# A graph-attention and expert layer: edge blocks read at fixed places, more source rows gathered early

## Chip, cores and metric

The kernel runs on one core of a Trainium2 chip. The metric is the device time of one execution in microseconds (us), as the median of several runs. PE is TensorE (PEld its weight loads), DVE is VectorE, ACT ScalarE, POOL GpSimd, SP SyncE; SP and ACT issue plain DMAs, POOL the indirect ones (gathers).

## The reference, cut to what matters

30000 nodes with 256 features, 510000 edges sorted by destination, each with a source and one of 8 types. The layer norm, one graph attention over the edges, and then a feed-forward part with a shared network and four gated experts:

```python
feat_all = einsum('ni,rhid->rnhd', layernorm(x), conv_weights)   # 8 types, 4 heads of 64
feat_src_e = feat_all[edge_type, edge_src]
feat_dst_e = feat_all[edge_type, edge_dst]
e = leaky_relu(sum(feat_src_e * attn_l[edge_type]) + sum(feat_dst_e * attn_r[edge_type]))
alpha = softmax of e over the edges of each destination
x = x + segment_sum(alpha[..., None] * feat_src_e, edge_dst) + h_bias
x = x + shared(layernorm(x)) + the two best of 4 experts, weighted
```

## The kernel before, in words

**Stage A** (lines 248 to 850) makes the features of all nodes. The nodes are 235 row tiles of 128. For each tile m, `norm` makes the layer norm (DVE statistics L164 and L165, a square root on ACT L167, reciprocal L168 and scaling L171 on DVE), `turn` transposes it on PE (L322, copied out at L324), and `group` multiplies it with the weights in five column groups (L335), whose results ACT or DVE copies out of PSUM into `fo` (L337); six PSUM banks stand between PE and these copies. `store` sends 1040 KB per tile to `feat` in DRAM, on SP (L351). `fo` has six buffers. Each feature row has 4 heads of 65 numbers, the last one being the source's part of the score. The parts for the destinations go to `er_d`.

The order of the work is written out by hand: the loop at L826 goes over the tiles and groups, and each engine runs its instructions in the order in which they are issued there. Between the groups, `aside` (L811) makes one step of a list of generators, `side` (L808): six steps per tile while it is busy with the edges. These generators are:

- `edge_records` (L369): reads src, type and dst in 10 chunks of 120 x 425 edges, writes one record of 4 numbers per edge (row, destination, type, "starts a node") to `rec` in DRAM, and then finds, for each of 252 blocks, the first edge at or after 2016 t that starts a new node (`lo_sb`) and that node's number.
- `places` (L613): for 21 batches of 12 blocks it loads the 2048 edges from each block's first edge on, with the position in a register (L629, L632; every third load is issued by ACT, the others by SP), sorts the 16 edges of each partition by source with MAX8 (L561), and makes `rko`: indices, masks, penalties and bits, written to `rk_d` (`records`, L541).
- `ranks` (L674): the three lowest sources of each partition make three lists of 128 rows per block, 756 lists in all. They are ranked by their highest row, in comparisons and in matmuls with 0/1 matrices (L724, L730).
- `expert_weights`: loads for stage B.

From tile 68 on, `early_rows` (L753) gathers these lists in the order of their ranks while the later features are still being made: one indirect DMA of 128 rows each (`fr`, L765, twelve buffers), and eight lists later a plain DMA to the list's own place in `stage` (L762, by turns from SP and ACT). `PACE` spreads them over tiles 68 to 231: 4.638 lists per tile. `early(i)` (L537) says how many tiles must be stored before list i may be gathered; a list above its bound raises a flag.

**Stage B** (L1020 to L1340) goes over the 252 blocks and one last block. `load` (L1055) fetches a block's records, `gather` (L1087) fills a ring of four blocks with 16 feature rows per partition: three come from `stage` in one DMA on SP, 13 in indirect DMAs on POOL (L1095). DVE and ACT make scores, the softmax and one-hot matrices; PE sums the weighted rows per destination (L1213). Beside it, step by step, the feed-forward part runs for groups of 512 finished nodes (class `Experts`, L852).

At the end stand loops that repeat the attention in a general way. They run only if the flag `bad` is raised: when a block's first edge, a node count, the order of dst or an early list's bound breaks what the blocks take for granted.

Of the kernel before, what the change touches and what calls it, by code (L numbers as in the profile page):

```python
# [65 lines left out]
EARLY = 3  # L66
# [7 lines left out]
def kernel(  # L74
# [41 lines left out]
    assert EP * EG * GPP == E and 512 <= N < 32768 and NBLK * S + 64 <= E  # L116
# [5 lines left out]
    rec = dram.tile([E + PAD, 4], I32, name="rec")  # L122
    dst16 = dram.tile([E + PAD], I16, name="dst16")
    rk_d = dram.tile([NBLK, P, OWN.n], I32, name="rk_d")
    rl_d = dram.tile([P, LAST.n], I32, name="rl_d")
    NI = EARLY * NBLK
# [10 lines left out]
    uns_d = dram.tile([EP], F32, name="uns_d")  # L137
# [9 lines left out]
    lo_sb = const.tile([1, KT * P], I32, name="lo_sb")  # L147
# [98 lines left out]
    with ExitStack() as cx:  # L246
# [54 lines left out]
        def norm(m):  # L301
            if m >= NT:
                return
            q, j = divmod(m, T)
            t = tiles[m] = {"xn": layernorm(xp, quad[q][:, j:j + 1], 1, "a", bufs=6)}
            if j == 1:
                load_x(q + 1)

        normed = [0]

        def norms(m):
            while normed[0] <= m:
                norm(normed[0])
                normed[0] += 1
# [54 lines left out]
        def edge_records(cl):  # L369

            srcv = src.rearrange("(p c) -> p c", p=EP)
            dstv = dst.rearrange("(p c) -> p c", p=EP)
            typv = edge_type_8.rearrange("(p c) -> p c", p=EP)
            recv = rec[0:E, :].rearrange("(p c) f -> p c f", p=EP)
            d16v = dst16[0:E].rearrange("(p c) -> p c", p=EP)
            gs = max(k for k in range(1, 6) if GPP % k == 0)
            nch = GPP // gs
            n = gs * EG
            uns = gp.tile([EP, nch], F32, name="uns")
            ep = cl.enter_context(tc.tile_pool(name="edges", bufs=2))  # L380
            edges = {}

            def fetch(c):
                if c == nch:
                    return
                c0 = c * n
                s_sb = ep.tile([EP, n], I32, name="s_sb")
                nc.sync.dma_start(s_sb, srcv[:, c0:c0 + n])
                t_sb = ep.tile([EP, n], I32, name="t_sb")
                nc.sync.dma_start(t_sb, typv[:, c0:c0 + n])  # L390
                d_sb = ep.tile([EP, n + 1], I32, name="d_sb")
                if c:
                    nc.sync.dma_start(d_sb, dstv[:, c0 - 1:c0 + n])
                else:
                    nc.vector.memset(d_sb[:, 0:1], -1)
                    nc.sync.dma_start(d_sb[:, 1:], dstv[:, :n])
                    with nc.allow_non_contiguous_dma(reason="one edge of each partition, once"):
                        nc.sync.dma_start(d_sb[1:EP, 0:1], dstv[0:EP - 1, EC - 1:EC])
                edges[c] = s_sb, t_sb, d_sb

            fetch(0)
            for _ in range(3):
                yield
            for c in range(nch):
                c0 = c * n
                fetch(c + 1)
                s_sb, t_sb, d_sb = edges.pop(c)
                yield
                r_sb = ep.tile([EP, n, 4], I32, name="r_sb")
                nc.vector.scalar_tensor_tensor(r_sb[:, :, 0], s_sb, float(R), t_sb, op0=ALU.mult, op1=ALU.add)  # L410
                nc.gpsimd.tensor_copy(r_sb[:, :, 1], d_sb[:, 1:])
                nc.gpsimd.tensor_copy(r_sb[:, :, 2], t_sb)
                yield
                nc.vector.tensor_tensor(r_sb[:, :, 3], d_sb[:, 1:], d_sb[:, :n], op=ALU.not_equal)
                d16 = ep.tile([EP, n], I16, name="d16")
                nc.gpsimd.tensor_copy(d16, d_sb[:, 1:])
                yield
                dn = ep.tile([EP, n], F32, name="dn")
                nc.vector.tensor_tensor(dn, d_sb[:, 1:], d_sb[:, :n], op=ALU.is_lt)
                nc.sync.dma_start(recv[:, c0:c0 + n, :], r_sb)  # L420
                nc.sync.dma_start(d16v[:, c0:c0 + n], d16)
                yield
                nc.vector.tensor_reduce(uns[:, c:c + 1], dn, AX.X, ALU.max)
                yield
            cl.close()
            pad = gp.tile([P, PAD // P, 4], I32, name="pad")
            nc.gpsimd.memset(pad, 0)
            nc.gpsimd.memset(pad[:, :, 1], -1)
            nc.gpsimd.memset(pad[:, :, 3], 1)
            padd = gp.tile([P, PAD // P], I16, name="padd")  # L430
            nc.gpsimd.memset(padd, -1)
            zx = gp.tile([P, D], F32, name="zx")
            nc.gpsimd.memset(zx, 0.0)
            yield
            nc.sync.dma_start(rec[E:E + PAD, :].rearrange("(p u) f -> p u f", p=P), pad)
            nc.sync.dma_start(dst16[E:E + PAD].rearrange("(p u) -> p u", p=P), padd)
            for j in range(2):
                nc.sync.dma_start(er_d[N + j * P:N + j * P + P], zx[:, :R * H])
            yield


            WN = 64
            FAR = float(1 << 23)
            dw = gp.tile([P, KT, WN + 1], I32, name="dw")
            nc.gpsimd.memset(dw, -1)
# [3 lines left out]
            first = gp.tile([P, KT], F32, name="first")  # L449
# [4 lines left out]
            for k in range(KT):  # L454
                nc.vector.tensor_scalar(first[:, k:k + 1], irow, float(S), float(k * P * S), op0=ALU.mult,
                                        op1=ALU.add)
# [19 lines left out]
            nc.vector.tensor_add(lof[:, 0, :], lof[:, 0, :], first)  # L476
            nc.vector.tensor_scalar_min(lof[:, 0, :], lof[:, 0, :], float(E))
            nc.vector.tensor_scalar(lof[:, 1, :], lof[:, 1, :], 0.0, float(N), op0=ALU.max, op1=ALU.min)
            yield
            lor = gp.tile([1, KT * P], F32, name="lor")  # L480
            nr = gp.tile([1, KT * P], F32, name="nr")
# [9 lines left out]
            nc.vector.tensor_copy(lo_sb, lor)  # L491
# [5 lines left out]
            unm = gp.tile([EP, 1], F32, name="unm")  # L497
            nc.vector.tensor_reduce(unm, uns, AX.X, ALU.max)
            yield
            with nc.allow_non_contiguous_dma(reason="one number of each partition, once"):  # L500
                nc.sync.dma_start(uns_d.rearrange("(p o) -> p o", o=1), unm)
            yield
            unr = gp.tile([1, EP], F32, name="unr")
            nc.sync.dma_start(unr, uns_d.rearrange("(o p) -> o p", o=1))


            two = gp.tile([1, 6], F32, name="two")
            gap = gp.tile([1, NBLK], F32, name="gap")
            for i, (row, most) in enumerate(((lor, CAP), (nr, P))):
                nc.vector.tensor_sub(gap, row[:, 1:NBLK + 1], row[:, :NBLK])  # L510
                nc.vector.tensor_reduce(two[:, i:i + 1], gap, AX.X, ALU.max)
                nc.vector.tensor_scalar(two[:, i:i + 1], two[:, i:i + 1], float(most), None, op0=ALU.is_gt)
                yield
# [3 lines left out]
            nc.vector.tensor_reduce(two[:, 4:5], unr, AX.X, ALU.max)  # L517
# [5 lines left out]
            nc.vector.tensor_reduce(two[:, 5:6], gap, AX.X, ALU.max)  # L523
# [6 lines left out]
        far = gp.tile([P, 2], F32, name="far")  # L530
        lists = gp.tile([P, NI], I32, name="lists")
        held = gp.tile([1, NI], I32, name="held")
        AT = 68 * NT // 235 if NT >= 100 else NT
        LAG, GI = 4, 21
        PACE = NI / ((NT - 4 - AT) * NG) if AT < NT else NI
# [5 lines left out]
        def records(kp, rc, lay, o, b0, n, order):  # L541

            u, of, ob = lay.u, o.bitcast(F32), o.bitcast(BF16)
            FL = [P, n, u]
            dst0 = rc[:, :, 0:1, 1]
            kw = kp.tile([P, n, u], F32, name=f"kw{u}")
            nc.vector.tensor_tensor(kw, rc[:, :, :u, 1], dst0.to_broadcast(FL), op=ALU.subtract)
            nc.gpsimd.tensor_copy(spans[:, b0:b0 + n], kw[:, :, u - 1])
            nc.gpsimd.tensor_copy(ends[:, 2, b0:b0 + n], rc[:, :, 0, 1])
            kk = kp.tile([P, n, u], F32, name=f"kk{u}")  # L550
            nc.vector.tensor_scalar(kk, kw, 0.0, float(K - 1), op0=ALU.max, op1=ALU.min)
            vi = kp.tile([P, n, u], I32, name=f"vi{u}")
            if order:
                key = kp.tile([P, 2, n, u], F32, name=f"key{u}")
                nc.vector.scalar_tensor_tensor(key[:, 1], rc[:, :, :u, 0], float(K), kk, op0=ALU.mult, op1=ALU.add)
                nc.vector.tensor_scalar_mul(key[:, 0], key[:, 1], -1.0)
                yield
                half = kp.tile([P, 2, n, 8], F32, name=f"half{u}")
                for b in range(n):
                    for i in range(2):  # L560
# [46 lines left out]
            for i, v in enumerate((4, 2, 1)):  # L607
                nc.vector.tensor_scalar(bits[:, :, i], ty, float(v), None, op0=ALU.is_ge)
                if v > 1:
                    nc.vector.tensor_single_scalar(ty, ty, v - 1, op=ALU.bitwise_and)  # L610
# [962 lines left out]
```

## Time and profile before

| | us |
|---|---|
| median of 3 runs | 6174.72 (6170.01 to 6176.68) |
| profiled execution | 6156.64 |
| its span, first to last instruction | 6155.0 |
| PE busy | 5745.5 (93%) |
| DVE busy | 4483.9 (73%) |
| POOL busy | 3996.1 (65%) |
| ACT busy | 3448.8 (56%) |
| stage A's gathers L765 | 756, from 608.2 to 1821.9 |
| stage B's gathers L1095 | 3294, from 1857.6 to 6017.7 |
| last matmul of stage A ends | 1852.1 |

The page gives busy times over the whole span, the span in 40 slices, the DMA queues, the chain that ended last and the costliest groups of instructions. The stages have different limits, so the table of windows (busy time of each engine in a stretch) and the waits of a stretch are of more use than the whole span's shares. An engine's idle time says nothing by itself; what matters is which wait ends last in a stage.

### The profile page before, as it was taken

To read this page: it belongs to the slowest core of one execution; us is meant where nothing else is said; L and a number is where in the kernel's file an instruction comes from. 1 tells how busy PE (TensorE), PEld (TensorE's weight loads), DVE (VectorE), ACT (ScalarE), POOL (GpSimd) and SP (SyncE) were. 2 spreads that over 40 slices of the span, in tenths; PEclk is the share of its full clock that TensorE was granted. 3 is DMA by queue.
4 is the path that set the end of the run, shared out by engine and by line. 5 is a ranking of instruction groups with operands and counts; after the bars stand their busy time and mean duration, and the time that the engine had idled before them with its cause. 6 is when DMAs were issued, how large, how long until landed. Compare 5 with 4: busy or idle time off the path is not lost. (4 is left out here: it accounts for less than half of the span.)

```text
span 6155.0 us, 91629 instructions
## 1 busy us (share of the span) xinstructions
PE 5745.5 (93%) x21807; PEld 3671.0 (60%) x21808; DVE 4483.9 (73%) x12808; ACT 3448.8 (56%) x8892; POOL 3996.1 (65%) x4365
## 2 busy tenths in 40 slices
PE   8789999999995899999999999999999999999998
PEld 4445555555553566666666666666666666666665
DVE  5673333333336888888888888888888888888884
ACT  3232222222224677677776677677677776677764
POOL 2230456566657777777777777777777777777770
PEclk9999999999997899999999999999999999999999
DMA  7574899999985666666666656665666656656551
GB/s 255 178 242 163 302 334 337 336 335 336 333 310 164 172 174 174 175 172 171 176 173 176 174 171 173 174 174 170 177 172 175 175 171 176 174 170 176 174 169 38
DMA packets 750202, 1257.46 MB, mean 204 GB/s; under 512 B 160453, under 2 KB 566017, under 8 KB 719441
## 3 DMA queue, kind: packets, MB, share of 16 engines
q0 software_dynamic: 194400, 539.40, 32.0%
q1 hardware_dynamic: 487681, 658.52, 31.5%
q10 hardware_dynamic: 67568, 53.54, 2.7%
q8 instruction: 180, 2.95, 0.2%
q14 instruction: 373, 3.06, 0.1%
HBM read 806.71 MB, written 444.28 MB: 203 GB/s over the span
## 5 line engine op out<-in xcount | busy, mean ns | idle before, releaser
L1095 POOL DMA_INDIRECT ft<-feat,rk x3294 | 3157.8, 959 | 1037.9 <-issue 381.7
L1213 PE MATMUL po<-ft,oh 128*128 128x260 f32 x8100 | 2160.2, 407 | 0.0
L1213 PEld LDWEIGHTS po<-ft,oh 128*128 128x128 f32 x8100 | 1540.3, 200 | 561.4 <-issue 272.4
L335 PE MATMUL ps<-w,xT 128*128 128x448 f32 (+1 forms) x4700 | 1736.8, 524 | 69.3 <-ACT fo L337 37.0
L335 PEld LDWEIGHTS ps<-w,xT 128*128 128x128 f32 x4700 | 882.0, 192 | 778.7 <-issue 614.4
L1149 ACT ACTIVATE oh<-icol,rk 128x128 f32<-128x128 f32 x4050 | 1334.8, 390 | 0.0
L1206 DVE TENSOR_TENSOR ft<-ft,p 128x768 f32<-128x768 f32 x1518 | 1278.8, 853 | 2.7 <-ACT ft L1199 2.7
L765 POOL DMA_INDIRECT fr<-feat,lists x756 | 716.1, 947 | 644.6 <-DMA stage<-fr 305.6
L337 ACT COPY fo<-ps 128x448 f32<-128x448 f32 (+1 forms) x808 | 413.1, 528 | 1072.0 <-PE ps L335 577.5
L1150 ACT ACTIVATE oh<-oh 128x384 f32<-128x384 f32 x1518 | 740.3, 488 | 48.1
L1132 DVE COPY_PREDICATED ere<-rk,pe 128x512 f32<-128x512 int16 (+1 forms) x759 | 549.1, 723 | 187.3 <-ACT ere L1127 178.6
L1198 ACT ACTIVATE p<-e 128x64 f32<-128x64 f32 (+1 forms) x253 | 71.2, 281 | 852.0 <-DVE e L1193 851.8
L951 PE MATMUL ph<-xT,v 128*128 128x512 f32 (+1 forms) x944 | 446.7, 597 | 0.0
L324 DVE COPY xT<-ptr 128x256 f32<-128x256 f32 x181 | 76.9, 425 | 467.1 <-PE ptr L322 467.1
L337 DVE COPY fo<-ps 128x256 f32<-128x256 f32 (+1 forms) x367 | 192.3, 524 | 282.7 <-PE ps L335 262.8
L895 PE MATMUL ph<-ident,c_xn 128*128 128x128 f32 x470 | 141.4, 374 | 141.8 <-ACT c_xn L887 138.1
L1139 DVE COPY_PREDICATED ere<-rk,ere 128x256 f32<-128x256 int16 (+1 forms) x759 | 247.7, 326 | 17.4
L1102 PE MATMUL t<-ident,tops 128*8 128x128 f32 x506 | 100.6, 282 | 160.2 <-DVE tops L1163 160.1
L951 PEld LDWEIGHTS ph<-xT,v 128*128 128x128 f32 x944 | 170.5, 190 | 123.6 <-issue 113.1
L1013 PE MATMUL pf<-v,a 128*128 128x256 f32 x940 | 242.0, 380 | 0.1
L951 PE MATMUL ph<-xT,w 128*128 128x512 f32 (+1 forms) x472 | 230.0, 610 | 0.2 <-ACT xT L897 0.2
L1277 DVE SCALAR_TENSOR_TENSOR xt<-po,den,xt 128x64 f32<-128x64 f32 x1012 | 217.4, 277 | 9.0
(239 smaller groups left out, 6059.5 us busy)
## 6 DMA issues: line engine op xcount, KB each, us to landing
feat<-fo SPq DMA_DIRECT2D x234, 1040.0 KB
ft<-stage SPq DMA_DIRECT2D x252, 390.0 KB
ft<-feat,rk POOLq DMA_INDIRECT x3294
stage<-fr SPq DMA_DIRECT2D x378, 130.0 KB
stage<-fr ACTq DMA_DIRECT2D x378, 130.0 KB
xt<-in_x_dram SPq DMA_DIRECT2D x253, 128.0 KB
x_d<-xt SPq DMA_DIRECT2D x253, 128.0 KB
x<-x_d SPq DMA_DIRECT2D x58, 512.0 KB
```

The lines of the kernel that those rows point to most:

```text
L335: nc.tensor.matmul(ps, t["xT"][:, k, :], w[:, k, c0:c1], start=k == 0, stop=k == 1)
L337: eng(t["fo"][:, h0:h1, :HD], ps[:, :n].rearrange("p (a d) -> p a d", d=HD))
L765: nc.gpsimd.indirect_dma_start(out=fr, out_offset=None, in_=feat[0:min(early(i // GI * GI) * P, N) * R, :], in_offset=bass.IndirectOffsetO ...
L951: nc.tensor.matmul(ps[:, :self.w], lhs, rhs, start=i == 0, stop=i == len(pairs) - 1)
L1013: nc.tensor.matmul(pf[:M], self.a2[:, i, tok], v3[:, i, :], start=False, stop=False)
L1095: nc.gpsimd.indirect_dma_start(out=s.ft[:, u].rearrange("p h d -> p (h d)"), out_offset=None, in_=feat[:, :], in_offset=bass.IndirectOffse ...
L1132: nc.vector.copy_predicated(s.ere, s.mask[:, k - 1, :, None].to_broadcast(at), s.pe[:, k:k + 1].to_broadcast(at))
L1139: nc.vector.copy_predicated(s.ere[:, :, :n], s.bits[:, i, :, None].to_broadcast([P, s.u, n]), s.ere[:, :, n:2 * n])
L1149: nc.scalar.activation(s.oh[:, u, :], icol, AF.Abs, bias=s.nd[:, u:u + 1])
L1150: nc.scalar.activation(s.oh[:, u0:u1], s.oh[:, u0:u1], AF.Relu, bias=1.0, scale=-1.0)
L1206: nc.vector.tensor_mul(fc, fc, pc[:, :, None].to_broadcast([P, (u1 - u0) * H, HD]))
L1213: nc.tensor.matmul(s.po.rearrange("n h d -> n (h d)"), s.oh[:, u, :], s.ft[:, u].rearrange("p h d -> p (h d)"), start=u == 0, stop=u == s. ...
```

## The change

- `edge_records` and the records in DRAM go (they are made only inside the loops at the end). `ordered`, a new generator, reads src, type and dst of 12 blocks at a time directly, at fixed places: block t always reads the 2048 edges from 2016 t on, the destinations with one neighbour on either side. All these loads are issued by SP. It sorts the 16 edges of each partition and keeps the sorted values `vi` and the destinations `dk` (16 bit) in SBUF, and the lowest rows for the lists. `borders` finds the first nodes of the blocks, one step for every four of `ordered`.
- `ranks` comes next, before `places`. Its 0/1 selections are made per half of the columns (441) and used at once by two matmuls.
- `places` finishes the records afterwards, from `vi` and `dk`, in 28 turns of 9 blocks; flags that were read from the records are now compared from neighbouring destinations. `rk_d` is laid out by partition: a turn writes 4608 bytes per partition in one piece.
- Lists: four per even block and three per odd block, 882 in all, from tile 60 on and up to tile 233: 5.098 per tile. Stage B gathers 12 rows per partition of an even block and 13 of an odd one.
- The statistics of a row tile are made in three slots of the loop (sums at group 0, square root at group 1, reciprocal and scaling at group 3) instead of all at group 1. The double step of `aside` moves from group 3 to group 2.

```diff
-EARLY = 3
+EARLY = 7
+def firsts(b):
+    return b // 2 * EARLY + b % 2 * 4
...
-    rk_d = dram.tile([NBLK, P, OWN.n], I32, name="rk_d")
+    rk_d = dram.tile([P, NBLK, OWN.n], I32, name="rk_d")
-    NI = EARLY * NBLK
+    NI = firsts(NBLK)
...
         def norm(m):
+            nc.vector.bn_stats(st, xg)
+            nc.vector.bn_aggr(mv, st)
+            yield
+            nc.scalar.activation(rs, mv[:, 1:2], AF.Sqrt, bias=eps)
+            yield
+            nc.vector.reciprocal(rs, rs)
+            nc.vector.tensor_scalar(xn[:, 0], xg, mv[:, 0:1], rs, op0=ALU.subtract, op1=ALU.mult)
...
-        AT = 68 * NT // 235 if NT >= 100 else NT
+        AT = 60 * NT // 235 if NT >= 100 else NT
-        PACE = NI / ((NT - 4 - AT) * NG) if AT < NT else NI
+        PACE = NI / ((NT - 2 - AT) * NG) if AT < NT else NI
...
+        def ordered(cl):
+                s = kp.tile([P, GB, U], I32, name="s_in", bufs=3)[:, :n]
+                nc.sync.dma_start(s, window(src, b0 * S, n, U))
+                t = kp.tile([P, GB, U], I32, name="t_in", bufs=3)[:, :n]
+                nc.sync.dma_start(t, window(edge_type_8, b0 * S, n, U))
+                    nc.sync.dma_start(d, window(dst, b0 * S - 1, n, U + 2))
+                nc.vector.tensor_tensor(kw, d[:, :, 1:U + 1], d[:, :, 1:2].to_broadcast([P, n, U]), op=ALU.subtract)
+                nc.gpsimd.tensor_copy(dk[:, b0:b0 + n], d)
+                nc.vector.tensor_scalar(kk, kw, 0.0, float(K - 1), op0=ALU.max, op1=ALU.min)
+                nc.vector.scalar_tensor_tensor(row, s, float(R), t, op0=ALU.mult, op1=ALU.add)
+                nc.vector.scalar_tensor_tensor(key[:, 1], row, float(K), kk, op0=ALU.mult, op1=ALU.add)
+                        nc.vector.max(half[:, i, b], key[:, i, b])
...
+        def mixed(cl):
+            other = borders()
+            for i, _ in enumerate(ordered(cl)):
+                yield
+                if i % 4 == 3:
+                    next(other, None)
...
         def places(cl):
-                    eng, dma = (ACT, nc.scalar) if b % 3 == 2 else (SP, nc.sync)
-                    dma.dma_start(rc[:, b].rearrange("p u f -> p (u f)"),
-                                  bass.AP(tensor=r.tensor, offset=r.offset, ap=[[4 * U, P], [1, 4 * UW]]))
-            for k, (b0, n) in enumerate(batches):
+            for k, (b0, n) in enumerate(turns):
+                for i, _ in enumerate(records(kp, OWN, o, vi[:, b0:b0 + n], dk[:, b0:b0 + n], k, b0, n)):
...
         def ranks(cl):
+                for c in range(IC):
+                    place = rp.tile([P, half], F32, name="place", bufs=3)[:IS, :n]
+                    nc.vector.tensor_scalar(place, order[:IS, i:i + n], rank[:, c:c + 1], None, op0=ALU.is_equal)
+                    nc.tensor.matmul(pl, turn_r[:, c], place, start=c == 0, stop=c == IC - 1)
+                    nc.tensor.matmul(pn, number[:, c:c + 1], place, start=c == 0, stop=c == IC - 1)
...
-            side = [edge_records(cl), places(cl), ranks(cl), expert_weights()]
+            side = [mixed(cl), ranks(cl), places(cl), expert_weights()]
...
-                        norms(m + NORMED)
-                    for _ in range((2 if g == 3 else 1) if busy else g == 2):
+                    if g in (0, 1, 3):
+                        norm_part()
+                    for _ in range((2 if g == 2 else 1) if busy else g == 2):
...
         def gather(t):
-                i, n = EARLY * t, EARLY
+                i, n = firsts(t), firsts(t + 1) - firsts(t)
```

## Prediction

> **What bounds the kernel now.** I read the table of windows first, because the kernel has two stages with different limits and shares over the whole span mix them. Columns: window, its length, then busy time and count for PE, PEld, DVE, ACT, POOL, then granted PE clock, DMA share, GB/s.
>
> ```profile
> 0.00:193.00 193.00, 150.76 (x415) 78.53 (x417) 93.82 (x222) 53.55 (x160) 34.58 (x63) 0.92 0.68 222
> 193.00:453.00 260.00, 221.61 (x622) 114.76 (x620) 218.79 (x1180) 80.50 (x257) 84.41 (x211) 0.95 0.71 223
> 453.00:508.00 55.00, 51.75 (x153) 27.05 (x154) 23.67 (x53) 16.98 (x53) 2.73 (x38) 0.93 0.60 189
> 608.00:1852.00 1244.00, 1244.00 (x3744) 675.76 (x3742) 467.10 (x1510) 320.62 (x677) 716.08 (x756) 1.00 0.94 326
> 2000.00:6018.00 4018.00, 3789.42 (x15863) 2596.68 (x15862) 3502.13 (x9345) 2827.82 (x7377) 3048.93 (x3182) 0.95 0.60 173
> 6018.00:6155.00 137.00, 111.78 (x427) 68.57 (x425) 50.09 (x161) 59.72 (x130) 1.12 (x4) 0.91 0.08 28
> ```
>
> From 608 to 1852 PE is busy all the time at full clock: stage A (the feature matmuls) is PE's. From 2000 to 6018 PE has gaps and a clock of 0.95, while POOL shows 76%. Which of them leads is told by POOL's timeline (start, length, idle before) and by the groups of its gather line:
>
> ```profile
> 1949.81 0.94 POOL L1095 DMA_INDIRECT ft<-feat,rk  x1 [0.30 <-PE t L1182]
> 1951.06 0.95 POOL L1095 DMA_INDIRECT ft<-feat,rk  x1 [0.30 <-DMA ft<-feat,rk]
> 1952.31 1.12 POOL L1095 DMA_INDIRECT ft<-feat,rk  x1 [0.30 <-issue]
> ...
> L1095 POOL DMA_INDIRECT ft<-feat,rk x3294: 940/946/1262, 1857.6 to 6017.7; - x194
> ```
>
> The gap before each gather is 0.30 us whatever the view names as its releaser, so POOL waits for nobody: 3293 steps from 1857.6 to 6017.7 are 1.2633 us each, 13 of them 16.42 us per block. POOL's gathers bound stage B; PE runs dry behind them, and after a dry spell its clock drops. The kernel is stage A until 1857.6, then 3294 gathers, then a tail of 137 us.
>
> In stage A the timeline of PE shows one transposition per row tile, 7.31 us apart wherever nothing disturbs it:
>
> ```profile
> 57.88 0.38 PE L322 MATMUL ptr<-ident,a_xn 128*128 128x128 f32 x2
> ...
> 65.19 0.38 PE L322 MATMUL ptr<-ident,a_xn 128*128 128x128 f32 x2
> ```
>
> 235 tiles at 7.31 are 1718 us; PE ends at 1852, so 134 us are lost, all before 520. The starts of these transpositions place the loss: tiles 8 to 16 lose 11, tiles 17 to 19 35, tiles 20 to 47 (193 to 453, `places`) 56, tiles 48 to 53 (`ranks`) 22, of which 17 are its own matmuls; the first 47 us lose some 10. The waits say why, first 47 to 193, then 193 to 453 (total, times, longest):
>
> ```profile
> ACT a_rs L167 <- DVE a_mv L165: 97.1, 15, 16.1
> PE ps L335 <- ACT fo L337: 34.0, 8, 12.0
> ```
> ```profile
> ACT fo L337 <- DMA rcb<-rec: 107.7, 16, 9.6
> ACT a_rs L167 <- DVE a_mv L165: 40.9, 14, 5.2
> DVE a_rs L168 <- ACT a_rs L167: 34.9, 29, 7.7
> PE ps L335 <- ACT xT L324: 29.1, 12, 4.7
> ```
>
> ACT, which empties PE's banks, stands behind DVE's statistics and behind loads of `rcb` that it issues itself; in 193 to 453 DVE is busy 218.8 and waits 34.9 for ACT's square root, together 253.7 of 260. DVE sets that stretch.
>
> **The change, part by part.** Sums are against the profiled execution: 6156.64 us, span 6155.0. The median of the runs is 18 us above it; I move the sum onto the median unchanged.
>
> *Gathers of stage B.* 756 staged lists become 882, so 126 gathers leave L1095: 12.5 per block, 3168 in all. 126 x 1.2633 = 159 us off the queue that bounds. Next in line is PE. At full clock the 100 us windows of stage B hold 418 to 435 matmuls, against 397 on average (14704 in 3700 us); a block has 65.3, so PE needs 15.0 to 15.6 us where POOL will need 12.5 x 1.2633 = 15.79. DVE is busy 87%, 14.3 us of a block. POOL stays last, by a thin 0.2 to 0.8 us. Bounds of this gain: 0 (PE keeps 16.42) to 159; I take 159, as PE's dips follow its own dry spells. Stage reads grow from 390 to 455 KB per block, at a DMA share of 0.60; hidden.
>
> On the clock the trace has a row: after PE's 2.07 us wait for c_xn at 2687 its next pair takes 0.96 us instead of 0.47. The Trainium skill, "TensorE: Matmul & The Clock Gate", Part 1, lets the clock fall after an idle window of some 3.4 us. By that rule only the 4 to 6 us gaps would cost, and they go when POOL is faster; by the row the c_xn gaps cost as well and PE sits nearer to 15.8. The sum is 159 by either.
>
> *Early lists in stage A.* They run from tile 60 to 233 at 5.098 per tile, where it was 4.638. POOL then needs 5.098 x 1.25 = 6.4 of 7.31 us: room. DMA has less:
>
> ```profile
> 700.00:1800.00 1100.00, 1100.00 (x3312) 597.70 (x3311) 418.23 (x1355) 285.48 (x603) 661.00 (x698) 1.00 0.97 336
> ```
> ```profile
> GB/s 319 352 341 341 320 345 341 317 338 346 335 340 333 341 343 316 335 341 332 336 336 341 320 351 329 337 342 336 344 325 338 334 342 324 328 347 327 338 340 338
> ```
>
> A tile moves 1.212 MB (features out, x in, er out) and 0.266 MB per list: 2.447 MB in 7.31 us is 335 GB/s, the 336 shown. After: 2.570 MB, 351 GB/s. Slices of 27.5 us reach 352 and average 336. If 352 can be held, nothing is lost; if 336 is the ceiling, a tile takes 7.65 us and 173 tiles lose 58. I take the middle, 344: 7.47 us, 27 us lost; call it 30. A late list holds ACT (it issues half of the writes to `stage`, L762), ACT holds the copies L337, and PE's six banks fill.
>
> A ceiling is also on a page: the Trainium skill, "DMA: Bandwidth & Descriptors", Specifications, gives about 358 GB/s of HBM per core. By it 351 just fits and the sum would be 30 us lower; the share of 0.97 at 336 speaks for less.
>
> *Edge preparation.* Records written and read back go; src, type and dst are loaded directly as 3 x 252 x 128 = 96768 packets of 64 and 72 bytes. The trace's packet records have 38-byte packets at 10.9 ns and 128-byte ones at 12.7; at 11.5 that is 70 us of the 16 engines in some 21 tiles (154 us), beside feature stores of 43%. Bounds: 0 lost, or at 24 ns each (the 256-byte packets at the start) 145 us plus stores, 57 lost. I take 0: the near sizes lie close. The 84 loads on ACT's queue go, and with them its 107.7 us of waiting; all new ones stand on SP's queue, ahead of feature stores, which six buffers cover. `borders` now advances every fourth step, so its DMA round trips no longer stop DVE as at 140 to 190.
>
> Steps: 129 for sorting, 31 for `ranks`, 194 for `places`, six per tile: 59 tiles, where it was 48. Sorting costs DVE per tile: three tensor-tensor forms 0.50+0.45+0.43, two scalar forms 0.52, 24 MAX8 at 0.082, halves and low rows 0.53, sum 4.4, with the statistics (0.42+0.18+0.16+0.43) 5.6 of 7.31: PE leads. A turn of `places` (9 blocks, one tile), scaled from the rows of 12 blocks: 12 scalar forms at 0.23 to 0.28 (3.0), 9 small ones at 0.16 to 0.2 (1.7), four others 1.5: 6.2, with statistics 7.4. Against 7.31 that is 28 x 0.1 = 3 us, as long as the square root no longer stops DVE: sum and reciprocal now lie two slots apart, ACT's part between. If that cover fails, 1 us per tile comes back, 30 us.
>
> So: tiles 8 to 19 keep 15 of 46; `places` keeps 20 of 56 (3, the tail with `thr` 7, slip 10); `ranks` goes from 22 to 28 (28 products of 441 columns for 24 of 378, and PE now waits on DVE's selections one at a time, with the tile's own matmuls queued behind and ACT's copies behind those). Net 59 us gained; bounds 0 and 95.
>
> **Sum.** -159 + 30 - 59 = -188: 5969 against the profiled execution, 5987 on the median.
>
> **Rivals.**
> 1. *PE takes over in stage B.* For it: a margin of 0.2 to 0.8 us per block, c_xn gaps that halve the clock. Against: POOL never waits. If half is lost: -80 + 30 - 59 = -109, 6066. Chance 0.15.
> 2. *The early part gains nothing* (small packets, or DVE as slow as before): -159 + 30 = -129, 6046. Chance 0.10.
> 3. *No loss on DMA*: -218, 5957. Chance 0.12.
> 4. *Slower: DMA overload stops PE in every tile.* Lists land late, ACT blocks, PE pauses, the clock halves. To eat 218 us of gain each of 173 tiles must lose 1.26 us, 8.57 us per tile, which is 300 GB/s; from there on it is slower. At 1.5 times that loss the time is 6284. Against: 336 are held now. Chance 0.04, and 0.02 for landing within 0.2% either way.
> 5. *It doesn't do what it says*: a border over 32 edges, or a list over its bound, raises the flag, and the loops at the end repeat the attention: at least stage B's 4160 us more. From the inputs the largest border is 29 and the nearest list 9 tiles inside. Chance 0.02.
>
> **How the numbers follow.** The forecast has 0.55. Measurements of this kernel tell 0.2% (12 us) from no change. Faster: 0.55 + 0.15 + 0.10 + 0.12 = 0.92; within 0.2%: 0.02; slower: 0.06. The range runs from both good bounds (-159 - 95 + 0, 5921) to rival 1 with the DMA ceiling at 336 (-81, 6094).
>
> **What would show it.** Right: gaps before L1095's successor stay 0.30 us with 3168 of them; tiles in 193 to 450 near 7.5 us; no ACT wait for edge loads; DMA near 0.99 between tiles 60 and 233 and the last transposition some 30 us earlier than now. Wrong: POOL waiting on PE's `po` for whole microseconds; tiles above 7.6 us in the middle of stage A; PE waits on `place` beyond 10 us.

## The result, and the profile after

| | us |
|---|---|
| changed kernel, median of 4 runs | 31232.61 (31215.06 to 31247.23) |
| kernel before, same chip | 6172.36 (6168.76 to 6176.68) |
| ratio | 5.0598, 95% interval 5.051 to 5.0686 |
| forecast | 5987 (5921 to 6094) |

The change made the kernel five times slower. The table of windows of the changed kernel (columns as in the prediction) shows two parts:

```profile
1000.00:1780.00 780.00, 780.00 (x2349) 424.45 (x2348) 276.85 (x949) 190.22 (x423) 515.77 (x545) 1.00 1.01 351
...
2200.00:5800.00 3600.00, 3414.77 (x14293) 2340.21 (x14292) 3142.34 (x8391) 2544.21 (x6631) 2618.32 (x2736) 0.95 0.60 173
...
6200.00:31200.00 25000.00, 15283.82 (x76360) 13109.28 (x76360) 9776.35 (x25852) 1307.86 (x3689) 4875.17 (x4703) 0.70 0.15 39
```

Up to about 6070 us the profile is of the kind shown before; the timeline has the last store of the normal output at 6070.27. Then come 25000 us of another program: PE at 0.70 of its clock, DMA at 0.15. The costliest groups of the page name it:

```profile
L1506 POOL DMA_INDIRECT ft<-feat,rc x4700 | 4874.7, 1037 | 17661.7 <-SPq L1566 13542.8
...
L1543 PE MATMUL pb<-ident,e 128*128 128x128 f32 x37600 | 7024.1, 345 | 0.0
```

Lines 1506 and 1543 stand in the loops at the end, which run only if `bad` is raised. So it was raised. The 4700 gathers there fetch the rows of all edges a second time, one group of four after the other, with POOL idle 17662 us between them.

The normal part did not go as forecast either. Its gathers, and the waits from 2200 to 5800 us (total, times, longest):

```profile
L1119 POOL DMA_INDIRECT ft<-feat,rk x3168: 940/946/1266, 1796.1 to 5943.4; - x198
```
```profile
POOL ft L1119 <- PE po L1237: 277.2, 726, 3.4
...
PE ph L919 <- ACT c_xn L911: 116.1, 122, 2.1
```

There are 126 gathers fewer, as said, but they take 4147 us where 3294 took 4160. And POOL now waits for PE by up to 3.4 us, where no such wait exceeded 0.3 before. The prediction had listed this as a sign that it is wrong.

### The profile page after: what moved, and what is told of

Its sections match the earlier page's. It is cut to its first block, busy times and chain, and to the rows that moved or that the text cites. A ratio compares the mean times of both kernels' runs of the same rounds, so it can differ in the third digit from the quotient of the medians.

```text
span 31232.9 us, 358971 instructions
## 1 busy us (share of the span) xinstructions
PE 21050.5 (67%) x98275; PEld 16796.5 (54%) x98276; DVE 14295.1 (46%) x38991; ACT 4774.5 (15%) x12655; POOL 8885.5 (28%) x9179
## 3 DMA queue, kind: packets, MB, share of 16 engines
q0 software_dynamic: 420000, 1165.36, 13.7%
## 5 line engine op out<-in xcount | busy, mean ns | idle before, releaser
L1506 POOL DMA_INDIRECT ft<-feat,rc x4700 | 4874.7, 1037 | 17661.7 <-SPq L1566 13542.8
L1543 PEld LDWEIGHTS pb<-ident,e 128*128 128x128 f32 x37600 | 6832.9, 257 | 1222.1 <-issue 886.7
L1543 PE MATMUL pb<-ident,e 128*128 128x128 f32 x37600 | 7024.1, 345 | 0.0
L1540 PE MATMUL pb<-msk,identb 128*128 128x512 bf16 x4700 | 2294.1, 488 | 4810.2 <-DVE mc L1546 1927.0
L1522 PE MATMUL pe<-er,ohT 128*128 128x33 f32 x9400 | 1753.4, 333 | 3277.5 <-DVE ohT L1511 3127.3
L1522 PEld LDWEIGHTS pe<-er,ohT 128*128 128x128 f32 x9400 | 1662.1, 259 | 3547.4 <-DVE ohT L1511 3370.0
L1546 DVE TENSOR_REDUCE mc<-pb 128x4 f32<-128x2048 f32 x1175 | 2692.4, 2291 | 1476.9 <-PE pb L1543 1476.9
L1561 PE MATMUL po<-ft,oh 128*128 128x260 f32 x9400 | 3007.5, 476 | 430.4 <-issue 430.4
L1561 PEld LDWEIGHTS po<-ft,oh 128*128 128x128 f32 x9400 | 2318.8, 252 | 909.6 <-issue 444.1
L1237 PE MATMUL po<-ft,oh 128*128 128x260 f32 x8100 | 2163.8, 407 | 0.0
L1554 PE MATMUL pq<-mc,ohT 128*128 128x4 f32 x9400 | 1569.8, 290 | 627.8 <-DVE mc L1547 627.8
L1237 PEld LDWEIGHTS po<-ft,oh 128*128 128x128 f32 x8100 | 1544.6, 200 | 558.1 <-issue 282.9
```

Of the source, the lines that this page charges most:

```text
L1237: nc.tensor.matmul(s.po.rearrange("n h d -> n (h d)"), s.oh[:, u, :], s.ft[:, u].rearrange("p h d -> p (h d)"), start=u == 0, stop=u == s. ...
L1506: nc.gpsimd.indirect_dma_start(out=ft[:, u].rearrange("p h d -> p (h d)"), out_offset=None, in_=feat[:, :], in_offset=bass.IndirectOffsetO ...
L1522: nc.tensor.matmul(pe[:, u, :], ohT[:, u, :], er, start=True, stop=True)
L1540: nc.tensor.matmul(pb[:, h].rearrange("n u p -> n (u p)"), identb, msk.rearrange("n u p -> n (u p)"), start=True, stop=False)
L1543: nc.tensor.matmul(pb[:, h, u, :], e[:, u, h:h + 1].to_broadcast([P, P]), ident, start=False, stop=u == UG - 1)
L1546: nc.vector.tensor_reduce(mc, pb.rearrange("n h u p -> n h (u p)"), AX.X, ALU.max)
```

## The experiments

The line numbers of the kernels are those of the changed kernel, except in e2, e5 and e10, which are edits of the kernel before. A letter b or c behind a number means the same kernel put on a chip again. Some runs fell on chips on which the kernel before took 7065, 7128 or 7145 us instead of 6160 to 6172. They are called chips with pauses below, the others undisturbed; a ratio is always against the kernel before on the same chip.

### What raised the flag: e1 and e2

`places` loads the destinations of the last block into a tile `dl` that is first filled with -1, with one place behind the very last edge. The new test marks each destination that is smaller than the one before it, takes the largest mark over all places (`uns`) and puts it into the flag. The place behind the last edge keeps its fill value, and -1 is smaller than any destination. **Theory F**: this one place raises the flag on any input. Rival: a border or list really out of bounds, as rival 5 of the prediction had it.

e1_last_value:

```diff
-            nc.gpsimd.memset(dl, -1)
+            nc.gpsimd.memset(dl, 32000)
```

> The changed kernel with one constant altered: the place behind the very last edge (partition 127 of the last block's destinations) holds 32000 instead of -1. Theory F (one flag, always raised): the new comparison 'a destination is smaller than the one before it' covers this place, -1 is smaller than 29999, the flag is up for any input and the general loops at the end run; with 32000 they don't run and the time is where the changed kernel's last block ends, 6075 us in its trace, so 6075 to 6100. Rival G (another flag: a border over 32 edges, a list over its bound, a partition over more than four nodes): 31200 us as before. The computed result is the reference's either way.

Measured: 6086.29 us (6082.07 to 6088.3), before 6160.64 on that chip, ratio 0.9879 (0.9862 to 0.9895). One fill value had cost 25146 us, and neither a border nor a list is out of bounds.

e2_before_flag raises the flag in the kernel before, by a comparison that always holds:

```diff
-            nc.vector.tensor_scalar(two[:, 3:4], before_last, float(N - P), None, op0=ALU.is_ge)
+            nc.vector.tensor_scalar(two[:, 3:4], before_last, 0.0, None, op0=ALU.is_ge)
```

> The kernel before with its flag raised on purpose (the test of the node before the last block is compared with 0 instead of N-128), nothing else. Theory F: the loops at the end cost what they cost in the changed kernel, some 25150 us, less the 10 passes that make the edge records there (some 50 us): 31250 us. Rival: the loops are dear only because of the change (records of 3 numbers, made again): clearly less than 31000.

Measured: 31219.78 us, ratio 5.0699 (5.0614 to 5.0783). Its window at the end is that of the changed kernel:

```profile
6300.00:31200.00 24900.00, 15278.71 (x76303) 13093.47 (x76303) 9755.24 (x25798) 1317.03 (x3703) 4865.96 (x4682) 0.70 0.14 39
```

So the loops cost some 25060 us in the kernel before too. Theory F stands, and all further questions are put to e1: what the change is worth once it does what it says.

### Why 126 gathers brought nothing: e3, e4, e5, e7

e1 against before, by the profile: the first gather of stage B comes 65.3 us earlier (1857.6 to 1792.3), the gathers last 4150.6 us instead of 4160.1, the tail is 6 us longer. Of the 159 us priced for stage B, 10 came. Windows of e1, its gathers, and its waits from 2200 to 5700:

```profile
550.00:1050.00 500.00, 500.00 (x1506) 271.76 (x1505) 180.74 (x620) 120.83 (x273) 332.22 (x350) 1.00 1.00 357
1050.00:1750.00 700.00, 700.00 (x2108) 380.28 (x2107) 250.03 (x858) 172.03 (x384) 464.45 (x489) 1.00 1.00 352
2200.00:5700.00 3500.00, 3317.47 (x13873) 2270.97 (x13872) 3052.61 (x8152) 2468.89 (x6431) 2555.98 (x2659) 0.95 0.59 173
```
```profile
L1119 POOL DMA_INDIRECT ft<-feat,rk x3168: 942/949/1267, 1792.3 to 5942.9; - x198
```
```profile
POOL ft L1119 <- PE po L1237: 262.5, 710, 3.2
...
PE ph L919 <- ACT c_xn L911: 112.9, 118, 2.1
...
PE t L1126 <- DVE tops L1187: 64.7, 16, 4.1
```

A step is 1.3106 us now. **Theory P**: PE binds stage B, with its own pauses at `tops` and `c_xn` and the half clock after them; fewer gathers only make POOL wait. The rival: the gathers themselves became slower. It falls by the rows: one takes 949 ns in the middle, where it took 946, and what grew are the waits before them.

e3_lists_756 is e1 with three lists for every block, as before the change:

```diff
-EARLY = 7
+EARLY = 6
-    return b // 2 * EARLY + b % 2 * 4
+    return b // 2 * EARLY + b % 2 * 3
```

> As e1, but three lists per block instead of four and three: 756 early lists, 13 gathers per block in stage B. Theory P (PE's pauses and its halved clock set 16.4 us per block in stage B, the gathers only stood level with it): within 15 us of e1. Rival Q (gathers bound stage B and the 126 fewer were worth their 159 us): 150 us above e1.

Measured: 6093.38 us (6087.01 to 6100.8), ratio 0.9889 (0.9872 to 0.9905): 7 us from e1 with 126 gathers more. The gathers:

```profile
L1119 POOL DMA_INDIRECT ft<-feat,rk x3294: 940/946/1261, 1782.7 to 5956.6; - x194
```

The step is 1.2675, near the 1.2633 of before. Between 3168 and 3294 gathers their number does not set the time here.

The pauses were there in the kernel before as well, from 2200 to 5700:

```profile
POOL ft L1095 <- PE po L1213: 212.1, 696, 0.3
...
PE ph L895 <- ACT c_xn L887: 110.0, 117, 2.1
...
PE t L1102 <- DVE tops L1163: 73.1, 18, 6.1
```

In `Experts`, `scale` makes `c_xn` on ACT and `turn`, the very next step, transposes it on PE. e4_turn_later puts one empty step between:

```diff
-                    + [lambda k=k: self.turn(k) for k in range(2)] + [lambda: None]
+                    + [lambda: None] + [lambda k=k: self.turn(k) for k in range(2)] + [lambda: None]
```

> As e1, with one empty step between the scaling of the expert part's rows and their transposition, so that PE comes to c_xn a slot later. Theory P: the waits of PE for c_xn (116 us in 3600, each followed by 7 to 14 us at half clock) go, the clock rises from 0.95 to 0.98 or more, a block takes 15.8 us by POOL, and the whole is 120 to 160 us faster than e1. Rival D (DVE's or ACT's queue sets the block, PE only waits with it): within 20 us of e1.

Measured: 5970.79 us (5964.78 to 5977.96), ratio 0.9690 (0.9674 to 0.9706), 116 us under e1, a little short of the 120 to 160 expected. Again, on another undisturbed chip:

> The same kernel as e4 (value mended, turn one step later), put again on one chip with the next three, because the chip of the last call ran the kernel before at 7064 us. On a chip that runs the kernel before at about 6160 us both theories expect what e4 took, 0.969 of the kernel before, 5960 to 5982 us. On a chip with the pauses of the last call it is only the base for the other three.

e4b took 5967.64 us, before 6165.67, ratio 0.9687 (0.9666 to 0.9708). PE's waits for `c_xn` sum to 0.3 us where they were 112.9; those for `tops` are more, but the longest is 2.5 us instead of 4.1; POOL waits for `po` at most 0.9 us:

```profile
2200.00:5700.00 3500.00, 3333.52 (x14295) 2288.91 (x14296) 3147.44 (x8404) 2535.97 (x6627) 2621.96 (x2743) 0.98 0.61 179
```
```profile
L1119 POOL DMA_INDIRECT ft<-feat,rk x3168: 940/946/1260, 1792.2 to 5828.2; - x198
```
```profile
POOL ft L1119 <- PE po L1237: 232.2, 757, 0.9
PE t L1126 <- DVE tops L1187: 86.2, 50, 2.5
```

The same gathers take 4036.0 us, 114.6 less than in e1. Little of the gain is idle time: PE's gaps from 2200 to 5700 sum to 183 us in e1 and 166 in e4b. Most of it is the clock. In the records, PE is at half clock for 331 of these 3500 us in e1, in 29 spells of 6.8 to 13.7 us, and for 150 in e4b, in 43 spells, 42 of them of 3.4. Half of the difference is 90 us of lost work, 107 over all gathers; with 20 for the gaps that is 127 as an estimate, about what was won. One spell of each, e1 first, in windows of a few us:

```profile
2679.00:2685.00 6.00, 5.98 (x28) 4.67 (x28) 5.81 (x18) 3.13 (x9) 4.60 (x5) 1.00 0.64 186
2685.00:2689.40 4.40, 0.40 (x4) 0.30 (x4) 4.14 (x12) 1.88 (x4) 3.24 (x4) 1.00 0.58 184
2689.40:2703.00 13.60, 11.64 (x33) 8.06 (x32) 11.51 (x32) 12.62 (x31) 10.49 (x11) 0.50 0.60 170
```
```profile
2672.00:2675.50 3.50, 1.55 (x8) 0.97 (x8) 3.36 (x9) 3.01 (x7) 2.80 (x3) 0.99 0.63 204
2675.50:2679.00 3.50, 3.07 (x7) 1.85 (x6) 1.82 (x4) 3.46 (x9) 2.67 (x3) 0.52 0.39 106
```

In e1 PE stands still for 4 us at `tops` and then works at 0.50 for 13.6 us, with a pause of 1.93 us for `c_xn` inside the spell. In e4b the pause at the same place is 2.4 us and the spell 3.4 us.

Did the kernel before have the same bound, or did the change bring it about? e5 is the kernel before with the same empty step; e7 is e4 with 756 lists.

> The kernel before with the empty step of e4 alone (the transposition of the expert part's rows one slot later). Theory L (level: 13 gathers at 1.2633 us make 16.42 us per block whatever PE does): PE's waits for c_xn go and its clock rises, and the time stays within 15 us of the kernel before. Rival P1 (PE's pauses alone set stage B in the kernel before too): 100 us faster or more.

e5 fell on a chip with pauses: 7111.47 us, before 7064.59, ratio 1.0073 (1.0045 to 1.0102). Again, undisturbed:

> The kernel before with turn one step later, as in the last call. Theory G (in the kernel before, the gathers of 1.2633 us bound the second stage, PE is only about as long): within 15 us of the kernel before. Rival (PE's pauses at c_xn bound the kernel before too, and its gathers only follow): faster by 60 to 120 us, near 6050 to 6100 where the kernel before takes 6160.

e5b took 6139.49 us, ratio 0.9963 (0.9953 to 0.9972), 26 us under before: 11 more than the theory allowed, far from the rival's 60 to 120. By the profiles the gathers last 4155.6 us, 4.5 less than before, and the tail behind them is 12 us shorter; the rest is not placed.

> As e4, with 756 early lists, so 13 gathers per block. Theory L: without PE's pauses the gathers bound stage B again at 16.42 us per block, 4160 us in all where e4 took 4044; 100 to 120 us slower than e4. Rival (the 126 fewer gathers are worth nothing, the empty step did it all): within 20 us of e4.

e7 on the chip with pauses: 6978.72 us, ratio 0.9879 (0.985 to 0.9908). Again, undisturbed:

> e4 with 756 early rows as in the kernel before, so 3294 gathers instead of 3168. Theory P (the pauses at c_xn had taken the second stage over; with turn later they are gone and the gathers bind again): 126 gathers more at 1.2633 us, less the part of the last stretch that PE still holds (3168 steps of 1.2769 instead of 1.2633: 43 us), so 95 to 130 us slower than e4 in the second stage, and up to 15 less in the first: 6050 to 6095 us in all. Rival (PE alone binds the second stage in e4 as well): within 20 us of e4.

e7b took 6070.17 us, ratio 0.9853 (0.9832 to 0.9874), 102.5 us above e4b, where 95 to 130 were expected. The gathers of e5b and of e7b:

```profile
L1095 POOL DMA_INDIRECT ft<-feat,rk x3294: 940/946/1267, 1859.1 to 6014.7; - x194
```
```profile
L1119 POOL DMA_INDIRECT ft<-feat,rk x3294: 942/946/1266, 1781.7 to 5937.0; - x194
```

So the two edits need each other, and the four undisturbed times say it without any trace (the left column from a chip where before took 6160.64, the right one from 6165.67):

| us | `turn` as it was | `turn` a step later |
|---|---|---|
| 3294 gathers (e3, e7b) | 6093 | 6070 |
| 3168 gathers (e1, e4b) | 6086 | 5968 |

Fewer gathers alone gain 7, the later step alone 23, both 125. With 3294 gathers the queue of POOL binds (1.262 us a step in e5b and e7b), and PE's pauses fit beside it. With 3168 PE with its half clock needs just as long as POOL did, and only where that goes as well does the time fall: to 4036.0 us, 34 above the 3168 x 1.2633 = 4002 of POOL alone.

### Where stage A gained: e6, e10, e9

The starts of the transpositions of e1 place its losses against 7.31 us per tile as the prediction did for before. Lost in tiles 8 to 16: 10.6 before, 11.3 in e1; 17 to 19: 34.9 and 0; 20 to 47: 55.8 and 38.6 (all in 27 to 32, beside `ranks`); 48 to 53: 21.9 and 0; 54 to 65: 0 and 8.2. In sum 123.2 and 58.1: 65 us gained. Of the last 8.2, tile 65 alone loses 5.2, soon after the first lists leave: ACT stands behind a list's write, by its waits from 500 to 545, and with it the copies that PE needs. With 756 lists tile 65 loses as much (6.2 in e3), so it is not the larger number. Behind tile 65 nothing is lost.

```profile
ACT fo L367 <- DMA stage<-fr: 6.6, 1, 6.6
```

e6_norm_once is e1 with a tile's statistics in one go:

```diff
-                    if g in (0, 1, 3):
-                        norm_part()
+                    if g == 1:
+                        norms(m + NORMED)
```

> As e1, but the statistics, square root and scaling of a row tile all at group 1 as in the kernel before. Theory S (DVE is nearly full in the turns of the records, and each square root waited for costs it up to 1 us): tiles 33 to 61 rise from 7.31 to some 8.3 us, 20 to 40 us slower than e1. Rival (DVE has room in these turns): within 10 us of e1.

On the chip with pauses e6 took 7021.74 us, ratio 0.9935 (0.9904 to 0.9966). It was run again beside e10, the kernel before with the statistics in three slots and the double step of `aside` at group 2, and this chip too had pauses:

> e1 with a tile's statistics in one go at group 1 again, as the kernel before has them; everything else of the change stays. If the three slots give the early gain (prediction: 31 of 46 us in the tiles 8 to 19): 20 to 35 us slower than e1, near 6110 to 6120 where e1 takes 6086. Rival (the early tiles gain because the records are no longer built beside them, and the slots do little): within 8 us of e1, 6078 to 6094.

> The kernel before with the statistics of a row tile in three slots and nothing else of the change. If the slots give the early gain: 20 to 35 us faster than the kernel before. Rival (DVE's total there is what PE waits for, and slots move it without making it less): within 10 us of the kernel before.

e6b: 7083.1 us, before 7128.32, ratio 0.9943 (0.9926 to 0.9959). e10: 7112.89 us, ratio 0.9977 (0.9965 to 0.9988). Whole times can't be set beside e1, but up to tile 65 the tiles are steady on these chips too (e5 there loses within 2 us per stretch of what before loses). e6b loses 11.4 in tiles 8 to 16, 0 in 17 to 19, 38.8 in 20 to 47: e1's values. e10 loses 10.7, 29.8, 45.3 and 21.4, against 12.3, 35.3, 53.9 and 23.6 in e5. In the changed kernel the three slots gain nothing that these tiles show; in the kernel before, with the moved double step, they gain 18 by the tiles, 16 by the ratio, between what e10's theory and its rival expected. e6b's rival stands: the slots did not heal the early tiles. What is left is the work that is no longer done beside them (the records), which was not tried by itself.

e9_ranks_ahead makes the 0/1 selections of `ranks` four steps ahead of the products:

```diff
-                for c in range(IC):
-                    place = rp.tile([P, half], F32, name="place", bufs=3)[:IS, :n]
+                for c in range(IC + 4):
+                    if c < IC:
+                        p = chosen[c] = rp.tile([P, half], F32, name="place", bufs=5)[:IS, :n]
...
+                    if c >= 4:
+                        nc.tensor.matmul(pl, turn_r[:, c - 4], chosen[c - 4], start=c == 4, stop=c == IC + 3)
```

> e4 with the selections of the ranks made four steps ahead of the products that read them, with five buffers instead of three. In e1 the three tiles beside the ranks lost about 38 us, 26 of it as 28 products of about 0.9 us that wait for their selection each, and 11 in one wait for the keys. If DVE's selections are what PE waits for there: 15 to 26 us under e4, 5945 to 5956 us where e4 takes 5971. Rival (DVE's own total in these tiles, or the tiles' statistics queued behind the selections, sets the time): within 8 us of e4, or up to 10 slower, since the statistics of the next tiles come behind more selections.

Measured: 5969.68 us, ratio 0.969 (0.9668 to 0.9712), 2 us from e4b. The expected gain did not come; the timeline of e1 shows why:

```profile
254.87 1.81 PE L763 MATMUL ps<-place,turn_r 126*128 126x441 f32 x2 [10.76 <-issue]
...
267.17 1.01 PE L763 MATMUL ps<-place,turn_r 126*128 126x441 f32 x2
268.11 0.90 PE L764 MATMUL ps<-place,number 126*1 126x441 f32 x2
268.94 1.01 PE L763 MATMUL ps<-place,turn_r 126*128 126x441 f32 x2
269.88 0.90 PE L764 MATMUL ps<-place,number 126*1 126x441 f32 x2
```

The rows stand back to back: 0.9 us for one product (two records) is PE's own work, not a wait, and in e9, with the selections made ahead, the rows take the same 0.9. 14 such pairs of rows are some 26 us, an estimate of what no order of DVE's work takes away. What is left is the wait of 10.76 us, in which DVE makes the comparisons for the ranks. It comes to them late, by a wait of 7.5 us for the keys' way through DRAM, and e9 has that wait too:

```profile
DVE less L749 <- DMA keys<-key_d: 7.5, 1, 7.5
```

By the starts of the transpositions e9 does lose less in tiles 20 to 47, 33 us where e4b loses 38 (PE's wait for the first product is 5.96 us), and gives 2 back by tile 67.

### Four lists for each block: e8

e8_lists_1008 is e4 with `EARLY` at 8 (1008 lists, 3042 gathers), and with two tiles put into the room of others.

> As e4, with four lists in every block: 1008 early lists, 12 gathers per block. In stage A a tile then moves 2.764 MB, 378 GB/s at 7.31 us. Theory C (DMA is at its ceiling at the 352 GB/s of e1, share 1.00): a tile takes 7.8 us, stage A 80 us more; stage B gains at most 50 (POOL's floor falls to 15.2 us per block, PE's stays near 15.6): 30 to 80 us slower than e4. Rival (the ceiling lies above 378): stage A keeps 7.31 us per tile, and the whole is as fast as e4 or faster.

> e4 with 1008 early rows, four lists for each block, so 3042 gathers. If the queues hold the tile of 7.31 us above 352 GB/s and the gathers bind the second stage of e4: 126 gathers less at 1.2633 us, 159 us, less what PE then holds back; PE is within 43 us of them already, so 40 to 60 us under e4, 5910 to 5930. Rival (352 GB/s is the ceiling: the tiles from 66 on take 4 to 6 per cent longer, 1170 us of them, and PE binds the second stage): 45 to 70 us lost in the first stage, about 0 to 50 gained in the second, 5965 to 6040.

> The same kernel as e8 and e8b (e4 with four lists for each block, 3042 gathers), for a chip without pauses. If the queues hold the tile of 7.31 us above 352 GB/s and the gathers bind the second stage of e4: 40 to 60 us under e4, 5910 to 5930 where the kernel before takes 6160. Rival (352 GB/s is the ceiling and PE binds the second stage): 45 to 70 us lost in the first stage, 0 to 50 gained in the second, 5965 to 6040.

All three fell on chips with pauses: 7091.36 us and ratio 1.0025 (0.9998 to 1.0052); 7130.31 and 1.0001 (0.9975 to 1.0028); 7153.64 and 1.0012 (0.9998 to 1.0026). By the ratio e8 gains nothing there over the kernel before, where e7 with 756 lists is at 0.9879 on the first of these chips. On that chip tiles 66 to 89 alone lose 56 us in e8, 37 in e6 with 882 lists and 7 in e7 with 756, and e8c moves only 280 GB/s from 1050 to 1750. On an undisturbed chip it stays open; an estimate from e1's rows speaks against more lists: 5.8 per tile make 2.76 MB by the prediction's count of bytes, and at the 357 GB/s that e1 held a tile would take 7.7 us, some 70 us over 173 tiles.

## Why the prediction was wrong, step by step

- **The step that failed** is the last rival: "a border over 32 edges, or a list over its bound, raises the flag ... From the inputs the largest border is 29 and the nearest list 9 tiles inside. Chance 0.02." Two causes of the flag were worked out from the inputs, and both are out of the question, as e1 shows. A third, the comparison of neighbouring destinations that the change writes anew, does not appear in the prediction: the fill value behind the last edge decides it, not the inputs. The price, "at least stage B's 4160 us more", was a lower bound and no estimate; e2 shows 25060.
- **Gathers of stage B, -159.** "I take 159, as PE's dips follow its own dry spells" is wrong. The dips follow waits for DVE (`tops`) and ACT (`c_xn`), and they stayed when POOL had less to do (`c_xn` 110.0 us before, 112.9 in e1): -10 in e1. PE's 15.0 to 15.6 us per block were taken from windows at full clock; e1's step of 1.3106 us makes 16.4 per block, the bound of no gain. Rival 1 had the right mechanism with half the loss; nearly all was lost. "By the row the c_xn gaps cost as well" was the better reading. The Trainium skill, "TensorE: Matmul & The Clock Gate", Part 1, which wants an idle window of some 3.4 us before the clock falls, is not borne out here: spells of half clock came after single gaps of 2.07 us (before) and 2.4 us (e4b).
- **DMA in stage A, +30: measured 0 from the rate, 5 where the lists begin.** 352 GB/s are held for 700 us, and 357 for 500, with tiles of 7.31 us throughout; tile 65 loses 5.2 in the way that the prediction described, ACT held by a late list. The middle between 336 and 352 was no ceiling: 336 was all that was asked for. Rival 3 was right in this. The figure of about 358 in the Trainium skill, "DMA: Bandwidth & Descriptors", Specifications, agrees with these rows: 351 fitted under it, and the highest rate held is 357. That it is the ceiling no run on an undisturbed chip shows.
- **Early part, -59: measured -65.** Tiles 8 to 19 keep 11 (15 forecast), `ranks` 39 (28), `places` 3 at its end (20), tile 65 the other 5. The terms as written sum to 61, not 59: 31 + 36 - 6. The sum was near by luck of signs, and the reason given for the first, the three slots, is not what did it (e6b).
- **The sum.** Without the flag it would have been 6086 on its chip (before: 6161), 74 faster where the forecast had 188. With `turn` one step later it is 198 (e4b).

## What to carry to other kernels

When a change rewrites a guard, follow every place that feeds it, the fill values and the padding first: a guard that is always true costs what the whole slow path costs, whatever the fast path gains. Before you price work taken from the engine that binds, ask what the next engine's time is made of; where it is waits on third engines and the low clock after them, it won't shrink along, and a single empty step between producer and consumer may be worth more than the work removed. A transfer rate at a share of 0.97 may still be all that was asked for, and no ceiling.

## What the runs showed of the hardware

- **The half clock outlives its pause, and the length of the pause does not tell for how long.** In before a gap of 2.07 us at 2685.0 (by the records) is followed by 10.2 us at 0.5. From 2200 to 5700 the 16 spells of 13.7 us in e1 follow a gap of 4 us and hold a second one of 1.9; the other 13 are of 6.8 or 10.2 us after a single gap of 2.1, with none of 0.3 us inside. In e4b gaps of the same size, 2.1 to 2.5, are followed by 3.4 us (one spell of its 43 is longer), and nine spells come some 5 us after a gap of only 1.1 to 1.3. What sets the length is not shown.
- **Some chips pause by themselves.** Where the kernel before takes 7065 us, a gather of e5 still takes 949 ns in the middle and a DMA packet of 1040 bytes 47 ns, the same as on an undisturbed chip (946 and 47), but engines often stand still without a releaser that the trace knows. The gathers of e5 there, and what POOL waited for:

```profile
L1095 POOL DMA_INDIRECT ft<-feat,rk x3294: 943/949/1263, 1971.1 to 6964.1; - x194
its engine sat idle before it (us, times) until:
  issue: 656.5, 2010
  PE po L1213: 460.4, 492
  remote: 171.2, 120
```

A step is 1.516 us there. What pauses these chips was not found. More lists gain nothing on them: with `turn` a step later, 756 lists (e7) are at 0.9879 and 1008 (e8) at 1.0025 on one such chip.
